# Six-channel groups as two accumulated blocks of 32 partitions, their matmuls issued in rounds, in a fused conv, attention and expert kernel

## The chip, the cores and the metric

The kernel runs on one core of a Trainium2 chip. The metric is the device time of one launch in microseconds (us). The core has a matrix engine (TensorE, PE in the profile, with its weight loads listed apart as PEld), VectorE (DVE), ScalarE (ACT), GpSimd (POOL) and SyncE (SP), which here issues the transfers. Each engine works through its own instructions in order and waits on semaphores for the others.

## The reference, cut to what matters

Eight images of 128 channels and 36 x 36 = 1296 positions pass two layers. The first is a group norm, convolutions, an attention over positions, a tanh and a projection. The second, which fills most of the time, is an additive attention over the 1296 tokens of each image, followed by a gated set of experts:

```python
q = jnp.einsum('bld,ed->ble', x, Wq) + bq
k = jnp.einsum('bld,ed->ble', x, Wk) + bk
t = jnp.tanh(q[:, :, None, :] + k[:, None, :, :])
scores = jnp.einsum('bijd,d->bij', t, w) + bw[0]
attn = jax.nn.softmax(scores, axis=-1)
return jnp.einsum('bij,bjd->bid', attn, x)
```

For each pair of a query i and a key j this wants 128 tanh values, weighted by w and summed. Everything is float32.

## The kernel before, in words

**The scores as ratios of matmuls.** A tanh of a sum is a ratio of exponentials of q and k. The kernel takes channels in groups of five or six. The product of the denominators of one group is a sum over all sign patterns of its channels, 32 patterns for five channels and 64 for six, of an exponential of the query times an exponential of the key. So the denominator of a group, for 128 keys and 432 queries, is one matmul with 32 or 64 contracted rows (`kf`, the key features, as weights; `qf[:, 0]`, the query features, streamed), and its numerator another one with `qf[:, 1]`, which is `qf[:, 0]` times a weight per row. There are 16 groups of five and 8 of six. I call them fives and sixes. The features lie in eight blocks of 128 rows: blocks 0 to 3 hold four fives each, blocks 4 to 7 hold two sixes each (`sign`, lines 521 to 539, gives the patterns; `features` turns them into the projections `a_q` and `a_k`).

**Units and slots.** A unit is one image, one chunk of 432 queries and one tile of 128 keys; there are 8 x 3 x 10 of them, and for each image and chunk one short unit for the 16 keys left over. A full unit has 12 slots (`SLOTS`, line 49), each with two groups, so two PSUM banks: slots 0 and 1 are fives, slot 2 is sixes, and so on in threes. I call three slots of this kind a triple, and k counts the slot within the unit. In a slot of fives the two matmuls use rows 0 to 31 and 32 to 63, or 64 to 95 and 96 to 127, of a block; from slot to slot the half changes. In a slot of sixes they use rows 0 to 63 and 64 to 127 of a block. The short unit has two slots, put together by `REM_BANKS` (line 66) from matmuls that fill 32 output partitions each (line 968); its second slot has the sixes, with 128 rows each, half of which are zeroed by `pairs`.

**What is done per slot p** (main loop from line 1137): `denominators(p + 3)` issues the two matmuls of slot p + 3 into a pair of banks `d` (two such pairs exist), and ScalarE takes the logarithm of both (Ln, line 986). For fives with k divisible by three an exponential of minus that follows at once (line 989, 864 columns); for the two other slots of a triple, one exponential of 1728 columns follows the second Ln. So `lq` is one over the denominator, three slots ahead of its use. Then `numerators(p)` issues two matmuls into two banks `n`, from a pool of four that also serves all other matmul work. `terms(p)` multiplies n by `lq` on VectorE, into `rp` (line 1017), which GpSimd adds up (line 1026), or, for k in 1, 4, 7, 10, in place (line 1011), which VectorE adds up itself (line 1013).

On PE the order is thus d(p+3), n(p), d(p+4), n(p+1), and so on. As the lag is three, d and n of one step are both of fives or both of sixes, except around the short unit. d(p+3) may start when the Ln of slot p + 1 has freed its bank pair; n(p) may start when VectorE is done with the banks that it gets. Those of a six were last held by the first slot of the same triple.

**The other work** (the first layer and the keys of the next image, attention of the chunk before, gating) comes in generators that are given turns after slots 2, 5, 8 and 11 (`TURNS`, `matmul_turn`, line 1102), as far as a budget (`PACE`) allows. The query features of the next chunk are made the same way, one block at a time (`query_block`, line 702: a matmul, an exponential on ScalarE at line 712, a product on GpSimd at line 713), in the order `IN_TURN` and at the slots in `NEXT_AT`, without regard to the budget. Their tiles come from a ring of nine.

Of the kernel before, what the change touches and what calls it, by code (L numbers as in the profile page):

```python
# [3 lines left out]

# [6 lines left out]
F32 = mybir.dt.float32  # L11
AF = mybir.ActivationFunctionType
ALU = mybir.AluOpType
# [7 lines left out]
CH = 432  # L21
# [24 lines left out]
NF = 8  # L46
# [1 line left out]

SLOTS = []
for m in range(NF // 2):  # L50
    for i in range(2):
        half = (m + i) % 2
        SLOTS.append((m, [slice(64 * half + 32 * h, 64 * half + 32 * h + 32) for h in range(2)]))
    SLOTS.append((NF // 2 + m, [slice(64 * h, 64 * h + 64) for h in range(2)]))
NP = len(SLOTS)
IN_TURN = [m + i for m in range(NF // 2) for i in (0, NF // 2)]
LAG = 3
SHIFT = 6.5
DVE_PAIRS = (1, 4, 7, 10)
TURNS = (2, 5, 8, 11)  # L60
NEXT_AT = {k: IN_TURN[i : i + 2] for k, i in zip(TURNS, (1, 3, 5, 7))}
PACE = 370

HALVES = [slice(0, 64), slice(64, 128)]
REM_BANKS = [[(q + i, rows) for i in range(2) for rows in HALVES] for q in (0, 2)]
REM_BANKS.append([(NF // 2 + i, slice(0, 128)) for i in range(4)])
REM_SLOTS = [REM_BANKS[:2], REM_BANKS[2:]]


@with_exitstack
def kernel(
# [58 lines left out]
    with ExitStack() as loop, ExitStack() as score:  # L132
# [82 lines left out]
            pattern=[[C // G, G], [0, C // G]], channel_multiplier=-1,  # L215
        )

        pairs = const.tile([128, 2, 2], F32, tag="pairs", name="pairs")
        nc.gpsimd.memset(pairs, 0.0)
        for s in range(2):  # L220
            nc.gpsimd.memset(pairs[64 * s : 64 * s + 64, 1, s : s + 1], 1.0)
            for o in (32 * s, 64 + 32 * s):
                nc.gpsimd.memset(pairs[o : o + 32, 0, s : s + 1], 1.0)

        by_key = const.tile([128, 2, REM], F32, tag="by_key", name="by_key")
        for s in range(2):
# [297 lines left out]
        def signs():  # L524

            sign = big_tile("sign")[:, : NF * 128]
            nc.gpsimd.memset(sign, 0.0)
            for n, first, half in ((5, 0, sign[:, : NF * 64]), (6, FIVES, sign[:, NF * 64 :])):
                groups = NF * 64 >> n
                for r in range(n):  # L530
                    v = half.rearrange("p (g h b l) -> p g h b l", g=groups, b=2, l=2**r)
                    for bit, value in ((0, -1.0), (1, 1.0)):
                        w = v[:, :, :, bit, :]
                        nc.gpsimd.affine_select(
                            out=w, in_=w, compare_op=ALU.not_equal, fill=value, base=-first - r,
                            pattern=[[-n, groups], [0, 2 ** (n - 1 - r)], [0, 2**r]],
                            channel_multiplier=1,
                        )
            return sign

        feat = {}
# [127 lines left out]
        def keys(b, tiles):  # L669

            xT = prepared[b][1]
            yield matmuls(1)
            for t in tiles:
                o, n = KT[t]
                first = (b, t) == (0, order[0])
                if first:
                    kf_of[0] = kfp.tile([128, NF, 128], F32, tag="kf", name="kf")
                for q0 in (0, NF // 2):
                    some = slice(q0, q0 + NF // 2)
                    pk = aux("pk1").rearrange("p (q t) -> p q t", t=128)  # L680
                    for q in range(NF // 2):
                        bmm(pk[:, q, :n], a_k[:, (q0 + q) * 128 : (q0 + q + 1) * 128],
                           xT[:, o : o + n], start=True, stop=True)
                    yield TAKE
                    if first:
                        ks = kf_of[0][:, some, :]
                    else:
                        ks = kstp.tile([128, NF // 2, 128], F32, tag="ks", name="ks")
                    nc.scalar.activation(ks[:, :, :n], pk[:, :, :n], AF.Exp)
                    kd3 = kd[b][t].rearrange("p (q t) -> p q t", t=128)[:, some, :]  # L690
                    if n == REM:

                        for x in range(2):
                            nc.gpsimd.tensor_scalar(
                                ks[:, :, (x + 1) * n : (x + 2) * n], ks[:, :, :n],
                                pairs[:, min(q0, 1), x : x + 1], None, ALU.mult,
                            )
                        nc.sync.dma_start(kd3[:, :, : 2 * n], ks[:, :, n : 3 * n])
                    else:
                        nc.sync.dma_start(kd3, ks)  # L700
                    if q0 > 0:
                        made.add((b, t))
                    yield matmuls()
# [209 lines left out]
        def drain(*gens):  # L913
            for g in gens:
                for _ in g:
                    pass
# [11 lines left out]
        def banks(u, k):  # L928
            return 2 if units[u][2] < NKT - 1 else len(REM_SLOTS[k])
# [26 lines left out]
        def products(u, k, part, outs):  # L956

            b, c, j = units[u]
            kf = kf_of[u]
            if j < NKT - 1:  # L960
                q, rows = SLOTS[k]
                for h in range(2):
                    mm(outs[h][:, :CH], kf[rows[h], q, :], qf_of[b, c, q][rows[h], part, :],  # L963
                       start=True, stop=True)
                return
            for out, bank in zip(outs, REM_SLOTS[k]):
                for i, (q, rows) in enumerate(bank):
                    mm(out[32 * i : 32 * i + 32, :CH], kf[rows, q, :32],  # L968
                       qf_of[b, c, q][rows, part, :], start=True, stop=True)

        def denominators(p):

            if p >= len(slots):
                return
            u, k = slots[p]
            d = ps_d.tile([128, 2, 512], F32, tag="d", name="d")
            n = banks(u, k)
            products(u, k, 0, [d[:, h, :] for h in range(n)])
            g, o = group_of[p]
            if g == p:  # L980
                alone = p in ends
                lq_of[g] = lp.tile(
                    [128, 2 if alone else 4, CH], F32, tag="lq1" if alone else "lq", name="lq"
                )
            lq = lq_of[g]
            nc.scalar.activation(lq[:, o : o + n, :], d[:, :n, :CH], AF.Ln)  # L986
            if p in ends:
                some = lq[:, : o + n, :]
                nc.scalar.activation(some, some, AF.Exp, scale=-1.0)  # L989

        def numerators(p):
            ns = [ps_n.tile([128, 512], F32, tag="n", name="n") for _ in range(banks(*slots[p]))]
            products(*slots[p], 1, ns)
            return [ps[:, :CH] for ps in ns]

        def terms(p, ns):

# [128 lines left out]
            else:  # L1126
                first_of_all.append(new_block(0, 0, q))
        for p in range(LAG):
            denominators(p)
        drain(keys(0, order[1:3]))  # L1130
        prefetch(1)
        urgent.append(keys(0, order[3:]))
# [1 line left out]
        for p, (u, k) in enumerate(slots):  # L1134
            b, c, j = units[u]
            rem = j == NKT - 1
            if k == 0:
                prefetch(u + 2)
                if c == 0 and j == 1:
                    if b > 0:  # L1140
                        gates.append(gating(b - 1))
                    if b == NB - 1:
                        gates.append(residuals(4))
                    if b + 1 < NB:
                        background.extend(
                            (normal(b + 1), conv_keys(b + 1), layer0(b + 1), tokens(b + 1),
                             keys(b + 1, range(NKT)))
                        )
            take_turns(p, k)
            denominators(p + LAG)  # L1150
            ns = numerators(p)
            terms(p, ns)
            if pending and pending[0][0] <= p:
                exps(p, *pending.popleft()[1:])
            last = p + 1 == len(slots) or slots[p + 1][0] != u

            if j == order[-1] and u + 1 < len(units):
                for q in NEXT_AT.get(k, ()):
                    first_of_all.append(new_block(*units[u + 1][:2], q))
            elif j == order[-2] and last and u + 2 < len(units):  # L1160
                first_of_all.append(new_block(*units[u + 2][:2], IN_TURN[0]))
            behind_rem = k == 0 and u > 0 and units[u - 1][2] == NKT - 1
            matmul_turn(
                p, k == 1 if rem else k in TURNS or behind_rem,
                lanes[:1] if behind_rem else lanes,
            )
            if last and rem:
                first_of_all.append(rem_scores(p, u, live.pop("rem")))
            elif last:
                pending.append((p + 7, u, sums(u)))  # L1170
# [211 lines left out]
```

## Time and profile before

| what | us |
|---|---|
| median of three runs (lowest, highest) | 6142.53 (6138.93, 6143.06) |
| the profiled execution's own time | 6138.18 |
| its span, first to last instruction | 6136.4 |
| from the first to the last Ln (the score loop) | 5823 |
| PE busy (share of the span) | 5669.6 (92%) |
| ACT busy | 5331.3 (87%) |
| DVE busy | 4787.2 (78%) |
| POOL busy | 4595.9 (75%) |
| mean granted PE clock | 0.982 |

The profile is of one execution, recorded by the hardware. A PE record is one pass; a float32 matmul makes two of them, each with its weight load, so a slot of two matmuls has four d records and four n records. Where several passes run side by side in different rows of the array, each has its own record and the busy time counts them once. A row of the list of groups reads: line, engine, operation, output and inputs, shapes, number; then busy us and mean ns of one; then the idle time of that engine just before such instructions, and whom it waited for. The mark `64*128` on PE stands for 64 rows and 128 columns of the array.

### The profile page before, as it was taken

Reading aid. Unit: us, or ns where it says so; the run is one execution under the profiler, and the core shown is the slowest. Engines: PE = TensorE matmul, PEld = TensorE weight load, DVE = VectorE, ACT = ScalarE, POOL = GpSimd, SP = SyncE. Lnnn points to the kernel's source line nnn. Section 1 sums busy time; section 2 is a strip of 40 time slices with the busy share of each in tenths; the row PEclk is TensorE's granted clock in tenths of the full one; section 3 lists DMA queues with packets and bytes.
Section 4 is the critical chain, followed back from the end, with each engine's and each line's share of the span. In section 5 each row is a group of like instructions: output and inputs, shape, how many; then the busy total and the mean of one; then the engine's idle time right before and its main releaser. Section 6 shows DMA issues by size and latency. Waiting matters only on the chain.

```text
span 6136.4 us, 94187 instructions
## 1 busy us (share of the span) xinstructions
PE 5669.6 (92%) x33480; PEld 2924.0 (48%) x33480; DVE 4787.2 (78%) x9521; ACT 5331.3 (87%) x5851; POOL 4595.9 (75%) x2819
## 2 busy tenths in 40 slices
PE   7999999999999999999999999999999999988886
PEld 5554455544554445544445444454455544534433
DVE  4787878878788788877788777887878878788882
ACT  1999898998989989889998999899998998999990
POOL 4777777787778867778687777877777777777870
PEclk9999999999999999999999999999999999999997
DMA  1200021001110011100111001110011001110008
GB/s 44 73 34 22 25 75 39 20 25 33 67 38 20 26 47 52 37 24 26 59 37 42 22 20 65 40 37 22 25 67 47 21 25 33 57 49 26 28 20 297
DMA packets 151528, 270.95 MB, mean 44 GB/s; under 512 B 45648, under 2 KB 76752, under 8 KB 151056
## 3 DMA queue, kind: packets, MB, share of 16 engines
q1 hardware_dynamic: 151056, 264.92, 13.0%
q8 instruction: 264, 4.33, 0.3%
q14 instruction: 208, 1.70, 0.1%
HBM read 200.41 MB, written 64.19 MB: 43 GB/s over the span
## 4 chain that ended last, share of the span: by engine, by line
PE 54%; DVE 16%; ACT 15%; issue 11%; POOL 2%; DMA 1%; SPq 0%; DVEq 0%; ACTq 0%; POOLq 0%
PE d L963 18%; PE n L963 12%; ACT lq L986 11%; PE pa L286 7%; DVE rp L1017 7%; DVE n L1011 5%; PE pc L286 5%; PE s L286 3%; DVE accd L1013 2%; PE pq L286 2%; PE pk L286 1%; PE d L968 1%; PE n L968 1%; ACT e L1046 1%; DMA w<-in_weight_dram 1%
## 5 line engine op out<-in xcount | busy, mean ns | idle before, releaser
L1026 POOL TENSOR_TENSOR accp<-accp,rp 128x864 f32<-128x864 f32 x1440 | 2912.8, 2023 | 989.4 <-DVE rp L1017 946.2
L963 PE MATMUL d<-qf,kf 32*128 32x432 f32 (+1 forms) x11520 | 2791.6, 563 | 264.8 <-ACT lq L986 259.6
L963 PE MATMUL n<-qf,kf 32*128 32x432 f32 (+1 forms) x11520 | 3001.7, 556 | 28.4 <-DVE rp L1017 10.0
L986 ACT ACTIVATE lq<-d 128x864 f32<-128x864 f32 x2928 | 2481.1, 877 | 471.2 <-PE n L963 288.8
L1017 DVE TENSOR_TENSOR rp<-n,lq 128x432 f32<-128x432 f32 x3912 | 2182.0, 601 | 760.7 <-PE n L963 606.0
L989 ACT ACTIVATE lq<-lq 128x864 f32<-128x864 f32 (+1 forms) x1944 | 2495.9, 1284 | 61.6
L963 PEld LDWEIGHTS d<-qf,kf 32*128 32x128 f32 (+1 forms) x11520 | 1026.4, 185 | 1445.5 <-ACT lq L986 1106.0
L963 PEld LDWEIGHTS n<-qf,kf 32*128 32x128 f32 (+1 forms) x11520 | 1263.3, 186 | 700.1 <-issue 293.8
L1013 DVE TENSOR_TENSOR accd<-n,accd 128x432 f32<-128x432 f32 x1440 | 867.8, 603 | 24.7
L1011 DVE TENSOR_TENSOR n<-n,lq 128x432 f32<-128x432 f32 x1440 | 810.8, 607 | 58.3 <-PE n L963 36.8
L1024 POOL TENSOR_TENSOR accp<-rp 128x864 f32<-128x864 f32 x240 | 485.1, 2021 | 290.3 <-DVE rp L1017 287.7
L286 PE MATMUL pa<-xh,e 128*108 128x129 f32 x1920 | 254.8, 281 | 35.2 <-DVE accd L1013 28.0
L286 PEld LDWEIGHTS pa<-xh,e 128*108 128x108 f32 x1920 | 221.0, 174 | 129.9 <-DVE accd L1013 103.0
L1035 POOL TENSOR_TENSOR accd<-accp,accd 128x432 f32<-128x432 f32 x240 | 266.1, 1109 | 18.8
L1033 POOL TENSOR_TENSOR accp<-accp 128x432 f32<-128x432 f32 x240 | 264.7, 1103 | 11.9
L713 POOL TENSOR_SCALAR qf<-qf,cs_s 128x432 f32<-128x432 f32 x192 | 260.0, 1364 | 9.3 <-ACT qf L712 9.3
L464 POOL TENSOR_TENSOR tot<-tot,e 116x432 f32<-116x432 f32 x192 | 212.2, 1105 | 9.0 <-ACT e L473 4.6
L286 PE MATMUL s<-q,k 128*116 128x432 f32 x480 | 207.0, 547 | 8.1 <-DVE accd L1013 5.6
L473 ACT ACTIVATE e<-s 116x432 f32<-116x432 f32 x240 | 116.1, 520 | 99.3 <-PE s L286 98.1
L286 PE MATMUL pa<-e,vw 116*128 116x432 f32 x480 | 196.8, 532 | 0.5
L286 PEld LDWEIGHTS pk<-xT,a_k 128*128 128x128 f32 x1408 | 164.9, 193 | 54.2 <-DVE accd L1013 43.5
L1006 DVE TENSOR_TENSOR accd<-n,lq 128x432 f32<-128x432 f32 x240 | 144.1, 600 | 50.1 <-PE n L963 29.7
(213 smaller groups left out, 3796.2 us busy)
## 6 DMA issues: line engine op xcount, KB each, us to landing
kf<-kd SPq DMA_DIRECT2D x239, 512.0 KB
kd<-ks SPq DMA_DIRECT2D x158, 256.0 KB
w<-in_weight_dram SPq DMA_DIRECT2D x32, 1024.0 KB
wk_t<-wk_t_d SPq DMA_DIRECT2D x7, 768.0 KB
wv_t<-wv_t_d SPq DMA_DIRECT2D x7, 768.0 KB
wq_t<-wq_t_d SPq DMA_DIRECT2D x7, 768.0 KB
x<-in_x_dram SPq DMA_DIRECT2D x8, 648.0 KB
t<-tokd SPq DMA_DIRECT2D x96, 54.0 KB
```

The lines of the kernel that those rows point to most:

```text
L286: mm(out, lhsT, rhs, **kw)
L713: nc.gpsimd.tensor_scalar(qf[:, 1, :], qf[:, 0, :], cs_s[:, q : q + 1], None, ALU.mult)
L963: mm(outs[h][:, :CH], kf[rows[h], q, :], qf_of[b, c, q][rows[h], part, :], start=True, stop=True)
L986: nc.scalar.activation(lq[:, o : o + n, :], d[:, :n, :CH], AF.Ln)
L989: nc.scalar.activation(some, some, AF.Exp, scale=-1.0)
L1011: mult(ns[h], ns[h], lq[:, o + h, :])
L1013: nc.vector.tensor_add(live["d"], ns[h], live["d"])
L1017: mult(rp[:, h, :], n, lq[:, o + h, :])
L1024: nc.gpsimd.tensor_add(live["p"], live["r"], rp)
L1026: nc.gpsimd.tensor_add(live["p"], live["p"], rp)
L1033: nc.gpsimd.tensor_add(s[:, 0, :], s[:, 0, :], s[:, 1, :])
L1035: nc.gpsimd.tensor_add(d, s[:, 0, :], d)
```

## The change

The sixes no longer use 64 rows of one block. The 64 sign patterns of a six are cut in two by the sign of its sixth channel, 32 with minus in one block and 32 with plus in another: blocks 4 and 6 form a pair, and 5 and 7. A six is then two matmuls of 32 rows that add up in the same PSUM bank, and all matmuls of full units have 32 rows. A slot of sixes uses the half of the rows that its turn in the alternation gives, so that d and n of one step are always in opposite halves.

`products` becomes a generator that pauses after each block, `denominators` and `numerators` too, and the main loop runs both by turns (`in_rounds`). For fives the PE order stays d, d, n, n. For sixes it was d, d, n, n with 64 rows; it is now d, d, n, n of the first block, then d, d, n, n of the second, with 32 rows each.

The sixes' two blocks are needed together, so `IN_TURN` and `NEXT_AT` change: before, blocks were made for the next chunk as two after slot 2, two after 5, two after 8 and one after 11; now one after 2, one after 5, two after 8, two after 11 and the last after slot 2 of the first unit that uses the chunk. The first block in turn is made a unit earlier in both. In the short unit each of the four bank parts with sixes takes two matmuls of 64 rows in place of one of 128. The sign patterns of the sixes are written with 22 instructions in place of 12 in the set-up.

```diff
 SLOTS = []
 for m in range(NF // 2):
-    for i in range(2):
-        half = (m + i) % 2
-        SLOTS.append((m, [slice(64 * half + 32 * h, 64 * half + 32 * h + 32) for h in range(2)]))
-    SLOTS.append((NF // 2 + m, [slice(64 * h, 64 * h + 64) for h in range(2)]))
+    for blocks, half in (
+        ((m,), m % 2),
+        ((m,), (m + 1) % 2),
+        ((NF // 2 + m // 2, NF // 2 + 2 + m // 2), m % 2),
+    ):
+        rows = [slice(64 * half + 32 * h, 64 * half + 32 * h + 32) for h in range(2)]
+        SLOTS.append((blocks, rows))
 NP = len(SLOTS)
-IN_TURN = [m + i for m in range(NF // 2) for i in (0, NF // 2)]
+IN_TURN = [0, 4, 6, 1, 2, 3, 5, 7]
+NEXT_AT = {2: (4,), 5: (6,), 8: (1, 2), 11: (3, 5)}
...
-NEXT_AT = {k: IN_TURN[i : i + 2] for k, i in zip(TURNS, (1, 3, 5, 7))}
...
-REM_BANKS = [[(q + i, rows) for i in range(2) for rows in HALVES] for q in (0, 2)]
-REM_BANKS.append([(NF // 2 + i, slice(0, 128)) for i in range(4)])
+REM_BANKS = [[((q + i,), rows) for i in range(2) for rows in HALVES] for q in (0, 2)]
+REM_BANKS.append([
+    ((NF // 2 + m, NF // 2 + 2 + m), rows) for m in range(2) for rows in HALVES
+])
...
-            for n, first, half in ((5, 0, sign[:, : NF * 64]), (6, FIVES, sign[:, NF * 64 :])):
-                groups = NF * 64 >> n
-                for r in range(n):
...
+            for n, first, groups, top in ((5, 0, 16, None), (6, FIVES, 8, -1.0), (6, FIVES, 8, 1.0)):
+                part = sign[:, at - NF * 64 : at - NF * 64 + groups * 32]
+                at += groups * 32
+                for r in range(5):
...
             if j < NKT - 1:
-                q, rows = SLOTS[k]
-                for h in range(2):
-                    mm(outs[h][:, :CH], kf[rows[h], q, :], qf_of[b, c, q][rows[h], part, :],
-                       start=True, stop=True)
+                blocks, rows = SLOTS[k]
+                for q in blocks:
+                    for h in range(2):
+                        mm(outs[h][:, :CH], kf[rows[h], q, :],
+                           qf_of[b, c, q][rows[h], part, :],
+                           start=(q == blocks[0]), stop=(q == blocks[-1]))
+                    yield
                 return
             for out, bank in zip(outs, REM_SLOTS[k]):
-                for i, (q, rows) in enumerate(bank):
-                    mm(out[32 * i : 32 * i + 32, :CH], kf[rows, q, :32],
-                       qf_of[b, c, q][rows, part, :], start=True, stop=True)
+                for i, (blocks, rows) in enumerate(bank):
+                    for q in blocks:
+                        mm(out[32 * i : 32 * i + 32, :CH], kf[rows, q, :32],
+                           qf_of[b, c, q][rows, part, :],
+                           start=(q == blocks[0]), stop=(q == blocks[-1]))
+            yield
...
-        def numerators(p):
-            ns = [ps_n.tile([128, 512], F32, tag="n", name="n") for _ in range(banks(*slots[p]))]
-            products(*slots[p], 1, ns)
-            return [ps[:, :CH] for ps in ns]
+        def numerators(p, ns):
+            for _ in range(banks(*slots[p])):
+                ns.append(ps_n.tile([128, 512], F32, tag="n", name="n"))
+            yield from products(*slots[p], 1, ns)
+
+        def in_rounds(*gens):
+            for _ in zip_longest(*gens):
+                pass
...
-            denominators(p + LAG)
-            ns = numerators(p)
-            terms(p, ns)
+            ns = []
+            in_rounds(denominators(p + LAG), numerators(p, ns))
+            terms(p, [ps[:, :CH] for ps in ns])
...
+            elif j == order[0] and k == TURNS[0] and u > 0:
+                first_of_all.append(new_block(b, c, IN_TURN[-1]))
```

`denominators` gives way to `yield from products(...)` in the same place, ahead of its Ln, and `pairs` loses the form that it had for 64 rows.

More of the change, by code (lines that the diff above doesn't have):

```diff
@@ L2 @@
 from contextlib import ExitStack
-from itertools import chain
+from itertools import chain, zip_longest
 import concourse.bass as bass
@@ L216 @@
         )
-        pairs = const.tile([128, 2, 2], F32, tag="pairs", name="pairs")
+        pairs = const.tile([128, 2], F32, tag="pairs", name="pairs")
         nc.gpsimd.memset(pairs, 0.0)
         for s in range(2):
-            nc.gpsimd.memset(pairs[64 * s : 64 * s + 64, 1, s : s + 1], 1.0)
             for o in (32 * s, 64 + 32 * s):
-                nc.gpsimd.memset(pairs[o : o + 32, 0, s : s + 1], 1.0)
+                nc.gpsimd.memset(pairs[o : o + 32, s : s + 1], 1.0)
         by_key = const.tile([128, 2, REM], F32, tag="by_key", name="by_key")
@@ L527, in signs, with filled @@
             nc.gpsimd.memset(sign, 0.0)
-            for n, first, half in ((5, 0, sign[:, : NF * 64]), (6, FIVES, sign[:, NF * 64 :])):
-                groups = NF * 64 >> n
-                for r in range(n):
-                    v = half.rearrange("p (g h b l) -> p g h b l", g=groups, b=2, l=2**r)
-                    for bit, value in ((0, -1.0), (1, 1.0)):
[L533 to L538, printed above, removed]
+            def filled(w, value, first, pattern):
+                nc.gpsimd.affine_select(
+                    out=w, in_=w, compare_op=ALU.not_equal, fill=value, base=-first,
+                    pattern=pattern, channel_multiplier=1,
+                )
+            at = NF * 64
+            for n, first, groups, top in ((5, 0, 16, None), (6, FIVES, 8, -1.0), (6, FIVES, 8, 1.0)):
+                part = sign[:, at - NF * 64 : at - NF * 64 + groups * 32]
+                at += groups * 32
+                for r in range(5):
+                    v = part.rearrange("p (g h b l) -> p g h b l", g=groups, b=2, l=2**r)
+                    for bit, value in ((0, -1.0), (1, 1.0)):
+                        filled(v[:, :, :, bit, :], value, first + r,
+                               [[-n, groups], [0, 2 ** (4 - r)], [0, 2**r]])
+                if top is not None:
+                    filled(part.rearrange("p (g l) -> p g l", g=groups), top, first + 5,
+                           [[-n, groups], [0, 32]])
             return sign
@@ L695, in keys @@
                                 ks[:, :, (x + 1) * n : (x + 2) * n], ks[:, :, :n],
-                                pairs[:, min(q0, 1), x : x + 1], None, ALU.mult,
+                                pairs[:, x : x + 1], None, ALU.mult,
                             )
@@ L977, in denominators @@
             n = banks(u, k)
-            products(u, k, 0, [d[:, h, :] for h in range(n)])
+            yield from products(u, k, 0, [d[:, h, :] for h in range(n)])
             g, o = group_of[p]
@@ L1128 @@
         for p in range(LAG):
-            denominators(p)
+            drain(denominators(p))
         drain(keys(0, order[1:3]))
```

## The prediction

> **What bounds the kernel now.** I read the page first, then the groups with shapes kept apart, then two stretches of the timeline.
>
> ```profile
> PE 5669.6 (92%) x33480; PEld 2924.0 (48%) x33480; DVE 4787.2 (78%) x9521; ACT 5331.3 (87%) x5851; POOL 4595.9 (75%) x2819
> ...
> PE 54%; DVE 16%; ACT 15%; issue 11%; POOL 2%; DMA 1%; SPq 0%; DVEq 0%; ACTq 0%; POOLq 0%
> ```
>
> PE looks like the bound (first line) and is half of the chain that ended last (second). But the score loop lasts 5823 us, and in it ACT is busy for 5287 us, 91%. By shape:
>
> ```profile
> L986 ACT ACTIVATE lq<-d 128x864 f32<-128x864 f32 x2904 | 2468.5, 880 | 452.0 <-PE n L963 288.8 <-PE d L963 87.6 <-PE d L968 61.9
> ...
> L963 PE MATMUL d<-qf,kf 64*128 64x432 f32 x3840 | 972.2, 584 | 224.2 <-ACT lq L986 220.4
> ...
> L963 PE MATMUL n<-qf,kf 64*128 64x432 f32 x3840 | 892.8, 534 | 10.0 <-DVE rp L1017 10.0
> ```
>
> ACT stands still for only 452 us before its Ln. The 64-row d, which the change rebuilds, is what PE itself waits for: 220 us with PE idle until a Ln has freed a bank pair. So the triple has to be read in time. One without other work:
>
> ```profile
> 3068.84 0.87 ACT L986 ACTIVATE lq<-d 128x864 f32<-128x864 f32 x1
> ...
> 3069.74 0.92 ACT L989 ACTIVATE lq<-lq 128x864 f32<-128x864 f32 x1
> 3069.76 0.30 PEld L963 LDWEIGHTS d<-qf,kf 64*128 64x128 f32 x4 [1.59 <-ACT lq L986]
> 3069.76 1.00 PE L963 MATMUL d<-qf,kf 64*128 64x432 f32 x4 [0.90 <-ACT lq L986]
> ...
> 3070.57 1.65 ACT L986 ACTIVATE lq<-d 128x864 f32<-128x864 f32 x2
> 3070.59 0.89 PE L963 MATMUL n<-qf,kf 64*128 64x432 f32 x4
> ...
> 3072.26 1.64 ACT L989 ACTIVATE lq<-lq 128x1728 f32<-128x1728 f32 x1
> ...
> 3073.80 0.87 ACT L986 ACTIVATE lq<-d 128x864 f32<-128x864 f32 x1
> ```
>
> ACT runs without a gap and sets the period, 3073.80 - 3068.84 = 4.96 us. The first Ln ends at 3069.71, the six's d starts 0.05 later and ends at 3070.76, n follows behind it. The second of the merged pair of Ln, the six's, starts at 3071.34 by its own record: d was ready 0.58 us early. One with other work:
>
> ```profile
> 3166.49 1.11 DVE L1017 TENSOR_TENSOR rp<-n,lq 128x432 f32<-128x432 f32 x2
> ...
> 3167.04 0.30 PEld L963 LDWEIGHTS d<-qf,kf 64*128 64x128 f32 x4 [0.62 <-issue]
> 3167.04 0.99 PE L963 MATMUL d<-qf,kf 64*128 64x432 f32 x4
> ...
> 3167.87 0.89 PE L963 MATMUL n<-qf,kf 64*128 64x432 f32 x4
> ...
> 3169.20 0.18 PEld L290 LDWEIGHTS tp<-ident,t2T 128*108 128x108 f32 x2 [1.14 <-DVE accd L1013]
> ```
>
> Here the banks for the six's n are free only when the two VectorE products end (3167.60), 0.56 after d began, and the next matmul waits for VectorE, not for n. I tabulated the single records of the 884 triples that lie away from the short units (of 958 that the table of Ln has). In 523 the next triple's first Ln follows without idle: ACT sets the pace. In 361 it waits, 0.83 us on average.
>
> **What the Trainium skill says.** "TensorEngine Tiling (Array Packing)", Key Properties: changing the tiling mode drains the array. The trace agrees: where PE is the last to be ready, the first 64-row load comes 0.088 us after the last 32-row column has streamed, and its first pass 0.107 after that, 0.195 together; within one mode loads are pulled ahead and passes follow each 0.36 us. "TensorE: Matmul & The Clock Gate", Part 3 (What overlaps and what doesn't): matmuls in different rows run together, but begin and end in program order. The trace agrees on both: with fives, n begins 0.013 us after d in the median. Same page, the spec table: ScalarE is a strict queue, so a late Ln holds all behind it; the unbroken ACT rows above fit.
>
> **The change part by part.**
>
> *PE work of a six.* Before: two passes of 0.36 us for d, then two for n, both row halves in use. After: four for d in one half, four for n in the other. Both take 4 x 0.36 = 1.45 us. So nothing is saved in streaming. The doubled instructions (32 for 16, loads counted) go at the pace that fives show already: no cost. Without that cover it would be an issue cost on each six; nothing in the fives hints at one.
>
> *d comes later.* It now ends with n, 0.725 us after its old end (the distance of n's end from d's end is 0.72 to 0.73 in nine of ten triples). The least distance from a d's end to its Ln is 0.047. So the six's Ln is late by 0.725 + 0.047 - slack. In the triple above that is 0.77 - 0.58 = 0.19: it starts at 3071.53. The ring first Ln, d, six's Ln, exponential, next first Ln is closed, so each such period becomes 4.97 + 0.19 = 5.16. The next wait is the six's Ln for its d. Where the score's exponential (L1046) lies between, slack is 1.13 and nothing is lost.
>
> *Mode switches go.* d of the six can be loaded ahead behind fives. That gains up to 0.195, but no more than d had already been free: over all triples 0.062 on average, since most d wait for ACT. Behind other work with 128 rows a switch remains. The one from the six to the next fives falls where that d has slack.
>
> *ACT-paced triples, sum.* Taking slack, gain and any idle time of each of the 523: mean loss 0.150, 78 us.
>
> *n's banks are wanted earlier.* n of the first block stands ahead of d of the second in the queue. A wait of n holds d's second block and all behind it. It reaches d only from 0.72 us on. n itself ends later by that wait, up to 0.72: the second bank's products end after d's start in half of the triples, mean wait 0.27 in the 361. After taking off the gain from switches and the time by which the following matmuls waited for something else anyway (as at 3169.20), 0.053 is left: 19 us. From below: the quartile of these triples is -0.087, -31 us; from above, 0.27 x 361 = 97.
>
> Both scaled by 958/884: (78 + 19) x 1.084 = **105 us**.
>
> *Short unit.*
>
> ```profile
> 2979.38 1.65 PE L968 MATMUL d<-qf,kf 64*32 64x432 f32 x16
> ...
> 2981.89 0.93 PE L968 MATMUL d<-qf,kf 128*32 128x432 f32 x8
> ...
> 2982.89 0.53 ACT L986 ACTIVATE lq<-d 128x432 f32<-128x432 f32 x1 [0.90 <-PE d L968]
> ```
>
> The second form becomes eight matmuls of 64 rows, so 16 passes as in the first line (1.65), 0.72 us longer for d and as much for n, in 24 units. ACT waits for this d in 23 of 24, so d's share is all on the path: 17 us. Of n's I take half, 9 us. **26 us**, from 17 to 35.
>
> *Set-up.* The sixes' sign patterns take 22 GpSimd selections for 12, over as many elements (20 x 128 + 2 x 256 = 12 x 256). The shortest of before took 0.52 us for 256, so what a selection costs without its elements lies between 0 and 0.52, and ten more cost 0 to 5. Most of the 12 took 0.6 to 2.2, so elements count: I take **1 us**. The chain of waits runs through them (4.94 us on it), so nothing hides it.
>
> *Moved query blocks.* 192 blocks as before, each a matmul of two passes, 0.60 us of ACT, 1.36 us of POOL, with no transfer; only turns change, from 2, 2, 2, 1 to 1, 1, 2, 2 and 1 in the next unit. They move past POOL's additions of 2 us too. The tightest is the last block: made after slot 2, wanted by d in step 5, three steps or 6 us later. That slack hides it: 0. If it fails, 24 chunks x 1 us = 24. The evener turns could give back as little: 24 x 0.45 = 11.
>
> Sum: 105 + 26 + 1 = 132. The profiled execution took 6138.2, so 6270; it lay 4.3 below the median, so **6275 us**, 2.2% slower.
>
> **The rivals.**
>
> *n's banks decide (slower still).* If the late n is passed on in full, 97 instead of 19, and the switch gain doesn't come (mean loss 0.189 for 0.150, 99 instead of 78): 196 x 1.084 + 35 + 5 = 252, **6395**. For it: n waits in half of the triples. Against: the matmul behind n mostly waits for VectorE.
>
> *Mode switches decide (faster).* If 0.195 came back in each of the 361 triples in which ACT waits, and ACT's ring had room for d's delay: 361 x 1.084 x 0.195 = 76, less 26 for the short units, **6093**. For it: PE's 92%, and 0.62 us of load-queue idleness put down to issue ahead of 64-row loads. Against: in 502 of the 884 d starts within 0.1 us of the Ln that frees its banks. It decides only where a six's d has more than 0.77 us of slack, or PE has some 0.2 us more to win than ACT lets through.
>
> *Hidden (no change).* ACT takes up the 0.19 in idle time elsewhere, and the short units hide theirs: **6145**. Against: 370 of the 523 lose more than 0.1 us, with ACT unbroken behind it.
>
> *A small part only.* Half of the ACT loss and the lower end of the short unit: 39 x 1.084 + 17 = 59, about **6200**.
>
> **How the numbers follow.** Forecast (6215 to 6330) 0.57; small part (6155 to 6215) 0.13; n's banks (6330 to 6400) 0.18; within 0.2% (about what a measurement of this kernel can tell from no change) 0.05; mode switches 0.07. Slower: 0.57 + 0.13 + 0.18 = 0.88. The range drops the faster and unchanged cases and the edges of the outer ones: 6180 to 6390.
>
> **What would show it.** Right: the six's d ending with n; a wait of ACT before the six's Ln, about 0.19 in quiet triples, whose period is 5.16; PE's total streaming unchanged; some 0.7 us more before the second Ln of short units. Wrong: quiet triples still at 4.97, or periods of crowded triples (6.2 on average now) falling by 0.1 or more.

## The result

| | us |
|---|---|
| before, median of four runs (lowest, highest) | 6140.73 (6127.24, 6143.06) |
| changed, median of four runs (lowest, highest) | 6311.26 (6309.73, 6315.92) |
| ratio, 95% interval | 1.0284 [1.0266, 1.0301] |
| changed, profiled execution (its span) | 6310.85 (6309.1) |
| score loop, start of the first Ln to start of the last: before, changed | 5822, 5992 |

The change makes the kernel 2.8% slower; the forecast was 2.2% (6275 us). First the page of the changed kernel: busy time by engine, and the chain that ended last by engine.

```profile
PE 5836.8 (93%) x41544; PEld 3184.2 (50%) x41544; DVE 4795.5 (76%) x9521; ACT 5399.0 (86%) x5851; POOL 4598.7 (73%) x2827
...
PE 67%; ACT 14%; issue 9%; DVE 8%; POOL 1%; DMA 1%; SPq 0%; DVEq 0%; POOLq 0%; ACTq 0%
```

PE's share of the chain has risen from 54 to 67%, while its share of busy time has hardly moved (92 to 93). That is what a late d looks like: PE is little busier, but others stand and wait for it. ACT's Ln as before, shapes kept apart (busy us, mean ns, then idle time of the engine ahead of them and who ended it):

```profile
L1003 ACT ACTIVATE lq<-d 128x864 f32<-128x864 f32 x2904 | 2541.0, 881 | 537.1 <-PE n L975 255.6 <-PE d L975 178.6 <-PE d L983 45.0
...
L1003 ACT ACTIVATE lq<-d 128x432 f32<-128x432 f32 x24 | 12.7, 530 | 37.3 <-PE d L983 37.3
```

ACT's wait for a d of full units has doubled, 87.6 to 178.6 us (first row). Taken apart by slot, the wait ahead of the six's Ln went from 48 to 223 us, with more than 0.05 in 734 of 958 triples, while that ahead of the first Ln fell from 309 to 240. The second row is the short unit's second Ln: its wait of 19.2 us became 37.3, which is the forecast 0.7 to 0.8 in each of 24.

The quiet triple, in the timeline of the changed kernel (start, duration, engine, line, what):

```profile
3289.27 0.87 ACT L1003 ACTIVATE lq<-d 128x864 f32<-128x864 f32 x1
...
3290.19 0.63 PE L975 MATMUL d<-qf,kf 32*128 32x432 f32 x2 [1.45 <-ACT lq L1003]
...
3290.21 0.63 PE L975 MATMUL n<-qf,kf 32*128 32x432 f32 x2
...
3291.00 1.85 ACT L1003 ACTIVATE lq<-d 128x864 f32<-128x864 f32 x2
...
3291.39 0.53 PE L975 MATMUL d<-qf,kf 32*128 32x432 f32 x2
3291.40 0.53 PE L975 MATMUL n<-qf,kf 32*128 32x432 f32 x2
...
3294.43 0.87 ACT L1003 ACTIVATE lq<-d 128x864 f32<-128x864 f32 x1
```

The six's d and n now start 0.02 apart and end together, at 3291.92. The merged pair of Ln takes 1.85 where it took 1.65; its second record starts at 3291.96, 0.04 after d's end. The period is 5.16 for 4.97, to the hundredth what the forecast derived. ACT's idle time in it is only 0.086; the other 0.1 is the overlap of two Ln that follow without a break, which is lost when the second has to wait. It appears as busy time of ACT, 5331 to 5399 us, so the wait alone understates the cost by half.

**Where the 173 us went.** I compared the two traces triple by triple, each from first Ln to next first Ln, in the classes of the forecast (527 triples after which, in the kernel before, ACT goes on to the next triple without idle time, 361 after which it waits, and what lies around the short units).

| class | forecast, us | measured, us |
|---|---|---|
| ACT set the pace | 78 | 92.2 (0.175 each) |
| ACT waited | 19 | 19.6 (0.054 each) |
| short unit itself, 24 | 17 | 18.2 (0.757 each) |
| triples beside short units | 17 (9, and 8 from the scaling) | 39.9 |
| ahead of the first Ln, and behind the last | 1 | 2.8 |

The sum is 172.7, the difference of the two spans. In the first row, 24 triples cost 16.0 us, about 0.7 each. They are those from slot 3 on in the first unit of each image and chunk, beside which the moved last query block is made. The others cost 76.2, or 0.152 each.

The fourth row is the large miss. In it the first triple after a short unit costs 45.6 us, the next 11.9, and the one ahead of the short unit gives back 17.6. The timeline of the changed kernel at one of them:

```profile
3061.94 1.67 PE L983 MATMUL d<-qf,kf 64*32 64x432 f32 x16
...
3063.71 0.53 ACT L1003 ACTIVATE lq<-d 128x432 f32<-128x432 f32 x1 [1.67 <-PE d L983]
...
3067.92 0.99 PE L975 MATMUL d<-qf,kf 32*128 32x432 f32 x4
...
3068.84 1.67 PE L983 MATMUL n<-qf,kf 64*32 64x432 f32 x16
...
3070.45 0.99 PE L975 MATMUL d<-qf,kf 32*128 32x432 f32 x4
...
3071.49 0.89 ACT L1003 ACTIVATE lq<-d 128x864 f32<-128x864 f32 x1 [2.56 <-PE d L975]
```

The first two rows are the forecast short unit: 16 passes for 8, and ACT waits 1.67 for 0.90. The others are not in the forecast. In this step d belongs to the next unit's first six and n to the short unit's second slot. That n yields only once, at its end, so the rounds issue the first block of d (3067.92), then all 16 passes of n (3068.84), then the second block of d (3070.45), for which ACT stands 2.56 us.

### The profile page after: what moved, and what is told of

Read it like the earlier page. It is cut to its first block, busy times and chain, and to the rows that moved or that the text cites. A ratio compares the mean times of both kernels' runs of the same rounds, so it can differ in the third digit from the quotient of the medians.

```text
span 6309.1 us, 110282 instructions
## 1 busy us (share of the span) xinstructions
PE 5836.8 (93%) x41544; PEld 3184.2 (50%) x41544; DVE 4795.5 (76%) x9521; ACT 5399.0 (86%) x5851; POOL 4598.7 (73%) x2827
## 4 chain that ended last, share of the span: by engine, by line
PE 67%; ACT 14%; issue 9%; DVE 8%; POOL 1%; DMA 1%; SPq 0%; DVEq 0%; POOLq 0%; ACTq 0%
PE d L975 27%; PE n L975 16%; ACT lq L1003 11%; PE pa L290 7%; PE pc L290 4%; DVE rp L1038 3%; PE s L290 3%; PE pk L290 3%; DVE n L1032 2%; PE pq L290 2%; PE n L983 1%; PE d L983 1%; DVE accd L1034 1%; DMA w<-in_weight_dram 1%; ACT e L1067 1%
## 5 line engine op out<-in xcount | busy, mean ns | idle before, releaser
L975 PE MATMUL n<-qf,kf 32*128 32x432 f32 x15360 | 3862.8, 559 | 44.2 <-ACT qf L723 25.1
L975 PE MATMUL d<-qf,kf 32*128 32x432 f32 x15360 | 3512.5, 552 | 304.7 <-ACT lq L1003 298.8
L1003 ACT ACTIVATE lq<-d 128x864 f32<-128x864 f32 x2928 | 2553.7, 878 | 574.3 <-PE n L975 255.6
L975 PEld LDWEIGHTS d<-qf,kf 32*128 32x128 f32 x15360 | 1413.1, 185 | 1542.9 <-ACT lq L1003 1054.4
L975 PEld LDWEIGHTS n<-qf,kf 32*128 32x128 f32 x15360 | 1689.5, 185 | 566.9 <-issue 135.9
L1054 POOL TENSOR_TENSOR accp<-accp 128x432 f32<-128x432 f32 x240 | 264.4, 1102 | 11.9
```

The source lines that it names most:

```text
L1054: nc.gpsimd.tensor_add(s[:, 0, :], s[:, 0, :], s[:, 1, :])
```

## The experiments

Each kernel's runs were taken beside runs of the kernel before on the same chip, and are read as a ratio to it. In what follows "the loop" is the time from first to last Ln in the trace of one execution.

**E1 and E2: the two halves of the forecast alone.** In E1 the sixes of full units take only the first block for d, and that block twice for n in place of both; in E2 n takes only the first block. The second block's share of the sums is left out. E2:

```diff
                 blocks, rows = SLOTS[k]
+                if part == 1:
+                    blocks = blocks[:1]
                 for q in blocks:
```

E1:

```diff
                 blocks, rows = SLOTS[k]
-                for q in blocks:
+                if part == 0:
+                    blocks = blocks[:1]
+                for i in range(len(blocks)):
                     for h in range(2):
-                        mm(outs[h][:, :CH], kf[rows[h], q, :],
...
+                        mm(outs[h][:, :CH], kf[rows[h], blocks[0], :],
...
```

> The changed kernel, but in full units the denominators of sixes take only the first of their two blocks, and the numerators take the first block twice, so that the second block is left out of the scores; n's passes and their places stay, d has two passes per bank as before the change and ends first again. Theory (d of the six comes too late for its Ln): quiet triples return from 5.16 to 4.97 us, the wait of ACT before the six's Ln goes from 223 us to about 50, and the short units lose part of their surplus, since no second block waits behind theirs: 6150 to 6190 us. Rival (n's banks are wanted too early, and hold the queue): n is issued as early as in the changed kernel, so 6280 us or more.

> The changed kernel, but in full units the numerators of sixes take only the first of their two blocks (the second is left out of the numerator); d keeps both blocks. A fourth of a six's passes is gone, but not one from the half that d uses. Theory (d's end sets the Ln): quiet triples stay at 5.16, the wait before the six's Ln stays near 220 us; n ends 0.7 us sooner, which only helps where VectorE waits: 6280 to 6315. Rival (n's load or its banks cost): 6180 to 6230.

Measured: E1 6243.85 beside 6133.36, 1.0181 [1.0164, 1.0198]. E2 6294.9, 1.0262 [1.0247, 1.0278], as expected. In E2 quiet triples stay at 5.16 and the six's Ln waits 233 us in all, so n's second block has no part in that. In E1 quiet triples are back at 4.97 and that wait is down from 223 to 27: the lateness of d is the whole of the 0.19. But E1 misses by over 50 us. Its row of the Ln, shapes apart:

```profile
L1005 ACT ACTIVATE lq<-d 128x864 f32<-128x864 f32 x2904 | 2465.7, 880 | 526.9 <-PE n L977 361.7 <-PE d L977 91.3 <-PE d L985 61.4
```

The wait for d has halved against the changed kernel, and the wait for "PE n" has grown from 255.6 to 361.7. ACT's total wait hardly moves, so in part of the triples the wait only changes its place. What each edit takes away is seen by class. The table has those triples during which the granted clock of PE is full in the traces of before, the changed kernel, E1 and E2 (from 3 us ahead of a triple's first Ln to the next first Ln), and by how much they are longer than before:

| class, number of triples | changed, us | E1, us | E2, us |
|---|---|---|---|
| ACT set the pace, 462 | 79.7 | 21.8 | 76.6 |
| ACT waited, 307 | 25.1 | 24.9 | -16.6 |

The two costs stand beside each other. d's second block costs where ACT sets the pace (58 us), n's where ACT waits (42 us), and together they make up nearly all of the 105 us of these triples. So E1 leaves n's part. In the 143 intervals that half the clock touches in one of the four traces, E1 is 33.7 us longer than before and E2 31.7, where the changed kernel is 1.8 shorter. So what E2 gains at full clock, 47 us with the short units, is mostly lost again in these (more on the clock at the end of the experiments).

**E3 and E4: the rounds.** E3 drops them beside short units only, E4 everywhere.

```diff
-            in_rounds(denominators(p + LAG), numerators(p, ns))
+            drain(denominators(p + LAG), numerators(p, ns))
```

(E3 makes this choice where p or p + LAG lies in a short unit.)

> The changed kernel, but without rounds in the steps in which one of the two slots belongs to a short unit: all of d, then all of n. Theory (in these steps the 16 passes of the short unit stand between the first and the second block of the next unit's six, so its d ends about 2.5 us late): 24 times 1.2 to 1.9 us, so 6265 to 6285. Rival (the short units lose only by their own doubled passes): 6305 to 6315, the same as the changed kernel.

> The changed kernel without rounds in all steps: d of both blocks, then n of both. Theory (d is late because its four passes go through one half of the rows, whatever is issued between them): quiet triples stay at 5.16 or above, and n now starts 0.72 us later in the other half, so PE has 0.7 us more per triple: about 361 triples times 0.6 more, less 40 at the short units, 6400 to 6520 us. Rival (the rounds themselves put n ahead of d's second block and make d late): d returns towards its old end, 6150 to 6200.

Measured: E3 6296.66, 1.0266 [1.0251, 1.0282]; E4 6293.6, 1.0264 [1.0249, 1.028]. Both intervals meet that of the changed kernel, so by the clock alone neither is apart from it. In the traces the loop is 12.5 us shorter in E3 and 18.0 in E4, and the place is plain: the first triple after a short unit costs 21.6 and 21.9 us where it cost 45.6. So the order found above is real and costs some 24 us there, of which 5 to 10 come back ahead of the next short unit. E3's saving is smaller than expected.

E4 was to tell whether matmuls start in program order, as the prediction held. There d's second block stands ahead of all of n, and in d's own rows, so n would have started about 0.72 us after d. The timeline of E4:

```profile
3274.62 0.63 PE L975 MATMUL d<-qf,kf 32*128 32x432 f32 x2 [1.45 <-ACT lq L1003]
...
3274.66 0.63 PE L975 MATMUL n<-qf,kf 32*128 32x432 f32 x2
...
3275.45 0.53 PE L975 MATMUL d<-qf,kf 32*128 32x432 f32 x2
...
3275.48 0.53 PE L975 MATMUL n<-qf,kf 32*128 32x432 f32 x2
```

n's first block runs from 3274.66, some 0.03 after d's, and 0.79 ahead of d's second block, which precedes it in the program. The array lets a matmul of free rows pass one that waits for its own rows. The triple takes 5.16 as with rounds. My theory of E4 falls by 100 us or more, and the rounds turn out to matter little for full units: away from the short units the triples are 105.1 us longer than before without them, 111.8 with them.

**E5 and E6: more room for d.** In the changed kernel the first slot of a triple has its exponential alone, and the six's Ln follows straight on the second slot's. E5 joins the first two slots in one exponential and leaves the six alone, which puts 1.64 us of ACT between; E6 makes the same exchange in the kernel before.

```diff
-            alone = not rem and k % 3 == 0
+            alone = not rem and k % 3 == 2
-            first = alone or (k == 0 if rem else k % 3 == 1)
+            first = alone or (k == 0 if rem else k % 3 == 0)
```

> The changed kernel, but the two slots of fives of a triple share one exponential of 1728 columns and the six has its own of 864; so 1.64 us of exponential stand between the first Ln and the six's in place of 0.92, and the six's d has 0.77 us more before its Ln. ACT does the same work. Theory (two costs that partly hide behind each other: d too late for its Ln, and n ending late because its passes follow each other in one half): quiet triples return from 5.16 to 4.97, the wait before the six's Ln falls from 223 us to under 60; but n's part, which the run with d of one block showed at about 79 us over full units, comes out from behind: about 20 to 45 us less than the changed kernel, 6262 to 6290. Rival (d's lateness is all of it): 90 to 110 us less, 6200 to 6220.

> The kernel before with the same exchange of exponentials as in the run before this one. Its six's d had 0.58 us to spare in quiet triples, so more slack should be worth little: 6120 to 6150, the same within 0.3%. If it is slower by as much as the changed kernel gains or more, the exchange has a cost of its own, and the two runs have to be read against each other.

Measured: E5 6269.82 beside 6133.73, 1.0221 [1.0205, 1.0238]; E6 6136.49, 1.0005 [0.9997, 1.0014]. The exchange costs the old kernel nothing and takes 0.6% off the new one. The wait ahead of the six's Ln falls from 223 to 88 us (under 60 was expected) and the class in which ACT sets the pace from 92 to 49. The short unit pays some of it back (28.8 us for 18.2, the longer exponential now stands ahead of it).

**E7: the query blocks' new turns, in the kernel before and with the old order of blocks.**

```diff
-NEXT_AT = {k: IN_TURN[i : i + 2] for k, i in zip(TURNS, (1, 3, 5, 7))}
+NEXT_AT = {2: (4,), 5: (1,), 8: (5, 2), 11: (6, 3)}
...
+            elif j == order[0] and k == TURNS[0] and u > 0:
+                first_of_all.append(new_block(b, c, IN_TURN[-1]))
```

> The kernel before with only the turns of the query blocks moved: one after slot 2, one after 5, two after 8, two after 11 and the last after slot 2 of the first unit that uses it, in the old order of blocks. In the trace of the changed kernel the triple from slot 3 of the first unit of a chunk is 16 us longer in sum, the last unit of a chunk gains some 12 against the units around it. Theory: the two cancel, within 10 us of the kernel before. Rival (the late block or the turns carry a good part of the loss): slower by 20 us or more.

Measured: 6145.94, 1.0021 [1.0015, 1.0028], 12 us for a forecast of 0; the loop of the traced execution is 5.8 longer. By unit, the first units of the chunks lose 13.4 us in all, in the triple from slot 3 on that the late block meets, and the last units gain 6.8.

**E8 to E11: what is left.** E8 joins E4 and E5. E9 adds to it that n of the full units' sixes takes one block; E10 adds instead that the short unit's sixes take one block for d and n; E11 adds both. E9 to E11 leave the second blocks' products out there. E9's edit is that of E2; that of E10, in the short unit:

```diff
                  for i, (blocks, rows) in enumerate(bank):
+                    blocks = blocks[:1]
                     for q in blocks:
```

> The changed kernel without rounds and with the exchanged exponentials. Without rounds lost 14 us at the short units and nothing elsewhere, so: 14 to 25 us below the run with the exchange alone, 6240 to 6275. Still slower than the kernel before, since n's passes and the short units' doubled ones remain. Rival (d alone): 6180 to 6205.

> The version without rounds and with the exchanged exponentials, and in full units the numerators of sixes take only their first block (the second is left out of the numerator). Theory (what is left in the full triples is n: a bank that VectorE frees late is followed by four passes in one half in place of two): the full triples' 63 us go to between 0 and -30, the short units' 44 stay: 6155 to 6190. Rival (what is left comes from PE's doubled instructions, the moved blocks or the short units): 6225 or more.

> The version without rounds and with the exchanged exponentials, and in short units sixes take only their first block in d and n (the second is left out of those scores), so eight passes per step as before the change. Theory: the 44 us around the short units go to about 5: 6200 to 6215. Rival (the steps around the short units lose by the next unit's six, not by the doubled passes): 6235 or more.

> Both of the two edits before together (the second block is left out of n in full units, and of d and n in short units). What is left of the change then: d of the six with four passes and slack for it, all full units in one tiling mode, the moved query blocks (13 us by the run with them alone) and the set-up (2 us). Theory: the costs add up, and the mode switches saved are worth some tens at most: 6115 to 6150, about the kernel before. Rival (a cost of the 32-row form that none of the runs has named): 6170 or more.

| kernel | median, us (before beside it) | ratio | loop, us | half clock in the loop, us |
|---|---|---|---|---|
| before | | 1 | 5822 | 137 |
| changed | 6311.26 (6140.73) | 1.0284 [1.0266, 1.0301] | 5992 | 85 |
| E4, no rounds | 6293.6 (6133.36) | 1.0264 [1.0249, 1.028] | 5974 | 85 |
| E8, E4 and six alone | 6247.2 (6133.73) | 1.0187 [1.0167, 1.0206] | 5930 | 113 |
| E9, E8 and n one block | 6241.37 (6133.74) | 1.0176 [1.0161, 1.0191] | 5920 | 297 |
| E10, E8 and short one block | 6219.18 (6133.74) | 1.0137 [1.0122, 1.0152] | 5899 | 116 |
| E11, all of these | 6188.74 (6133.74) | 1.0095 [1.0075, 1.0115] | 5861 | 246 |

E8 lies within its expectation. E10 comes near to its own: 28 us for the doubled passes of the short units, whose second Ln waits 19.4 us again:

```profile
L1004 ACT ACTIVATE lq<-d 128x432 f32<-128x432 f32 x24 | 12.7, 530 | 19.4 <-PE d L984 19.4
```

What E9 should take away is seen at one triple beside attention. In the kernel before:

```profile
3624.03 1.00 PE L963 MATMUL d<-qf,kf 64*128 64x432 f32 x4 [0.25 <-ACT lq L986]
...
3624.86 0.89 PE L963 MATMUL n<-qf,kf 64*128 64x432 f32 x4
...
3625.68 1.14 PE L286 MATMUL pa<-xh,e 128*108 128x129 f32 x8
```

The same one in E8:

```profile
3688.05 0.63 PE L975 MATMUL d<-qf,kf 32*128 32x432 f32 x2 [0.25 <-ACT lq L1003]
3688.08 0.97 PE L975 MATMUL n<-qf,kf 32*128 32x432 f32 x2
...
3688.55 0.52 PE L975 MATMUL n<-qf,kf 32*128 32x432 f32 x1
...
3689.26 0.88 PE L975 MATMUL n<-qf,kf 32*128 32x432 f32 x3
...
3690.07 1.14 PE L290 MATMUL pa<-xh,e 128*108 128x129 f32 x8
```

In E8 the loads and passes of n's second bank wait for VectorE, until 3688.43 by the single records, and then four passes follow one another in the same rows. The attention's first matmul (`pa`) comes 2.02 us after d's start for 1.65. Before, n had both halves of the rows when its banks came, and made up for them in two passes. In E9 that triple is back at 4.99 from 5.26 us, and the class in which ACT waited falls from +18.1 to -13.6 us, as expected. Yet E9 gains only 6 us on E8, their intervals overlap, and its expectation is missed: by the time alone it lies where its rival was put (6225 or more), and so does E11 (6170 or more). The granted clock suggests why. E9 in two stretches of 6.8 us (length, then busy us and number for PE, PEld, DVE, ACT and POOL, then PEclk, and the share and rate of DMA):

```profile
4512.50:4519.30 6.80, 6.61 (x34) 3.80 (x30) 6.63 (x15) 6.51 (x7) 4.50 (x5) 0.98 0.00 0
4519.30:4526.10 6.80, 6.80 (x32) 5.33 (x30) 5.60 (x11) 3.88 (x6) 6.72 (x5) 0.52 0.01 2
```

And two rows of its timeline in the second of them:

```profile
4520.01 0.92 PE L977 MATMUL d<-qf,kf 32*128 32x432 f32 x1
...
4522.48 0.89 ACT L1005 ACTIVATE lq<-d 128x864 f32<-128x864 f32 x1 [2.10 <-PE d L977]
```

At half the clock a pass takes 0.92 for 0.52, PE is called 100% busy, and ACT waits 2.10. The last column of the table sums such stretches: with n's passes removed they grow from 113 to 297 us, and every 2 us of them lose up to 1. That could be 92 us, more than what E9 and E11 miss by (some 50 and 40 from their expected ends). E1 (205 us) and E2 (239) show the same. No run takes the half clock away by itself, so this cause is argued from the traces and not shown.

The traces do show where the time is lost. Away from the short units, 764 triples run at full clock in the traces of before, E8 and E9. In these E8 is 51.2 us longer than before, and E9 1.1 shorter. For before, E10 and E11 it is 780 triples, of which E10's are 52.6 longer and E11's 0.1 shorter. So at full clock n's second block costs as much as E8 had left there, as the theory of E9 has it. In the 149 intervals that a half clock touches in before, E8 or E9, E8 is 12.3 us longer than before and E9 56.2. Whether the clock made these long, or long waits in them brought the clock down, stays open.

## Why the prediction was right, and where it was not

**Right.** The direction and its cause, that d comes later by the streaming of two more passes: its period of 5.16 was met, E1 takes it away and E5 makes room for it. The short unit's own 17 us (18.2). The class where ACT waited, 19 forecast and 19.6 measured. No issue cost for the doubled instructions shows: in quiet triples the passes follow each 0.36 us as before. "PE's total streaming unchanged" holds there (1.74 us for d and n, 1.72 before), but PE's busy time as a whole rose by 167 us: 35 are the short units' passes (24 x 2 x 0.72), and by E9, which is 94 us less busy than E8 (5727.0, 5821.3), most of the rest are passes of n that run alone after a wait.

**Mis-sized: "Of n's I take half, 9 us."** What lies beside the short units cost 40 us where that term and the scaling gave 17. I priced n of the short unit as 0.72 us on the following work and did not follow it through the rounds, which put all 16 of its passes between the two blocks of a d. The diff alone shows this: one generator yields once per block, the other once at its end. E3 takes 24 of the 45.6 us in the first triple behind them away.

**Right, though its class came out larger: "mean loss 0.150, 78 us".** The class lost 0.175 each, 92 us. But the 24 triples beside the moved block are in it with 16.0 us, and the others lose 0.152. In E7, where d is as before, the same 24 lose 13.4 us. So most of the 14 us too many belong to the next term.

**Wrong: the moved blocks' "That slack hides it: 0".** E7 gives 12 us, half the 24 that I had named for its failure, and places it where the last block is made.

**Wrong in its ground: "begin and end in program order".** So I read the Trainium skill, "TensorE: Matmul & The Clock Gate", Part 3 (What overlaps and what doesn't), and took n's start 0.013 behind d for agreement. E4's trace differs: n starts 0.79 ahead of an earlier matmul that waits for its rows. The trace before could have told, pass by pass: in a step of fives, d's first two passes start at 3008.82, n's first two at 3008.83, and d's other two, which belong to the earlier matmuls and wait for the same rows, only at 3009.29. So that an engine works through its instructions in order, as is said at the top, does not hold for PE where an instruction waits for rows.

It does hold where one waits for a semaphore, as the step "n's banks are wanted earlier" has it. The timeline of the changed kernel at one six:

```profile
771.79 0.99 PE L975 MATMUL d<-qf,kf 32*128 32x432 f32 x4
...
773.99 0.18 PEld L975 LDWEIGHTS n<-qf,kf 32*128 32x128 f32 x1 [0.22 <-DVE rp L1038]
...
774.00 0.63 PE L975 MATMUL d<-qf,kf 32*128 32x432 f32 x2
...
775.05 0.89 ACT L1003 ACTIVATE lq<-d 128x864 f32<-128x864 f32 x1 [1.58 <-PE d L975]
```

d's first block has gone through its rows 0.83 us after d's start, by the single records, but its second block begins 2.21 after it, right behind the first load of n's second bank, which VectorE frees late. Of 919 such steps at full clock, d's second block starts ahead of n's second bank in none, and is held by it for more than 0.05 us in 53, for 25.6 in all. In E4, where d's second block precedes n, it is never held, and yet the class in which ACT waited is no shorter (21.1 for 19.6). So the hold is real and costs little. What costs is the other half of that step, n itself ending later: by E8 and E9 n's second block, four passes in a row after a wait, is 32 us in that class, and without it 13.6 are gained. The forecast 19 for the two together was right.

**The rivals.** Mode switches bring little: the class in which they could pay is at -13.6 us in E9, where d is made room for and n is short, and 76 were asked. "Hidden" fell with the 170 us of the loop. "n's banks decide" had a right mechanism at about half its size: in the class in which ACT waited n's second block costs 42 us by E2, for 97 asked, and d's lateness costs beside it, in the other class.

**What stays open.** E11 still loses 39 us in the loop. E7's turns are some 6 to 12 of it, the short units and the two triples behind each 17.5 (9.0 in E6, which has the same exchange of exponentials); the rest, 10 to 16, is compatible with the 109 us more of half clock, which was not tried alone. No version here beats the kernel before; E6 equals it.

## What to carry to other kernels

Cutting a contraction into two accumulated halves on half the rows leaves the streamed work as it was but makes the result late by half of it: look for who waits for the first result (here ScalarE's next Ln, with 0.58 us of slack for 0.77), not at the engine's busy time. When two streams are issued by turns, list the order at every place where their lengths differ. And a cost that an experiment takes away can be eaten by another, here by stretches at a lower clock: compare such runs by class of step, and at the same granted clock, before you call the cost small.

## What was not expected of the hardware

- A matmul may start ahead of an earlier one that waits for other rows: by 0.79 us in E4, in quiet triples. It did not start ahead of an earlier one that waits for a semaphore: in the changed kernel d's second block was held up to 1.4 us with its rows free.
- Two Ln of 864 columns take 1.65 us together when they follow at once, 1.85 when a wait of 0.086 lies between.
- PE falls to half clock inside a kernel that keeps it 92% busy, for 3.4 us or a small multiple, and fewer passes bring more of it (113 to 297 us from E8 to E9, 116 to 246 from E10 to E11). The Trainium skill, "TensorE: Matmul & The Clock Gate", Part 1, puts the half rate down to an idle window of about 3.4 us. The length agrees; but of the 61 stretches in E9's loop 27 begin after 3.4 us in which the records show PE busy for 83% or more, so an idle window by these records isn't needed. Less busy windows do come before it more often: of those of that length at full clock, 34 of the 206 less busy ones are followed by half clock, and 27 of the 1440 others.
